# Experts' biases and layer 2's gamma and beta folded into the first product of a two-layer mixture-of-experts kernel, GELUs of 512 columns

## The chip, the cores and the metric

One core of a Trainium2 chip. The metric is device time in microseconds (us) of one execution; smaller is better. The kernel before takes 3586.99 us, the median of 14 runs (3571.68 to 3599.5).

## The reference

Sixteen batches of 512 tokens of width 128 go through six stages. Two kinds of feed-forward layer with 8 experts (each token goes to 2) come twice each, with attention between the first two and a state-space mixer ("mamba") between the last two. All is float32.

```python
x = x + 0.5 * _L0_ffn_ref(_layernorm(x), ...)      # call n = 0
x = x + _L0_attn_ref(_layernorm(x), ...)
x = x + 0.5 * _L0_ffn_ref(_layernorm(x), ...)      # call n = 1
x = x + 0.5 * _L1_ffn_ref(_layernorm(x), ...)      # call n = 2
x = x + _L1_attn_ref(_layernorm(x), ...)           # mamba
x = x + 0.5 * _L1_ffn_ref(_layernorm(x), ...)      # call n = 3

# _L0_ffn_ref, per expert (buf: the rows sent to it, at most a capacity)
h = gelu(einsum('ecd,edf->ecf', buf, W1) + b1, approximate=True)
ye = einsum('ecf,efd->ecd', h, W2) + b2
# _L1_ffn_ref: x is normalized once more inside, then
xn = (x - mu) * rsqrt(var + LN_EPS) * gamma + beta
h = gelu(einsum('bld,edh->eblh', xn, w1) + b1, approximate=False)
out_e = einsum('eblh,ehd->ebld', h, w2) + b2       # combined with the two gates; + x
```

D = 128 is the token width, F = 512 an expert's hidden width (NF = 4 pieces of 128), E = 8 experts. A row that comes out of a layer norm has a sum of zero, so its last number is minus the sum of the other 127.

## The kernel before

Each of the four expert calls n = 0 to 3 is cut into four groups of batches (`GROUPS`: 2, 5, 5, 4 batches, then 2, 4, 5, 5 twice, then 5, 5, 4, 2). A group is one `moe(...)` with these parts:

- `front(b)` (L551 and on) computes the norm's moments of a batch, the normalized and transposed rows, and the router's logits. `routes()` computes, for a whole group, to which slot of a DRAM buffer every row goes. `scatter(b)` (L657, L662) makes the normalized rows on POOL and sends them to `slots` by indirect DMAs, 8 for a batch.
- `blocks()` (L687 and on) runs over the slots in blocks of 256 rows (`BS`); a block belongs to one expert. A group of 2 batches has 15 blocks, of 4 batches 23, of 5 batches 27; 368 in all, 184 for each of the two layers. `fetch(i)` reads the block's expert number into a register and loads that expert's packed row `wb` (first weights, second weights, b1, b2; 1,156 numbers for each partition, L693) and the 256 rows `xs` (L697). `turned(xs)` transposes them on TensorE into `ps_b` (L709) and copies them out as `bl_xT`: on VectorE for layer 1 (L712), on ScalarE with gamma and beta as scale and bias for layer 2 (L714). The first product writes four pieces of 256 columns into two PSUM tiles `ps_h0` and `ps_h1` (L727). Four GELUs of 256 columns, each with its column of b1 as bias, make `hT` (L736). One block later, `second_product` multiplies `hT` with the second weights into `ps_b` (L676), VectorE adds b2 (`yo`, L681), and ScalarE's queue stores the result (L685).
- `back(b)` gathers the results by indirect DMAs on POOL (L775) and adds them to x on VectorE (L767).

`ps_b` is a single PSUM buffer: transposes of a block and second products of the block before alternate in it. `ps_h0` and `ps_h1` are single too. `wb` has three buffers, `xs` three, `hT` two.

At the start, SyncE's queue loads x, then packs both layers' weights in DRAM (`packed`, L419, from four inputs each), with the clearing of the four `slots` buffers (L407) between.

The mamba's `states(b)` (L960 and on) is 16 steps of two scans on VectorE (L978, L987), with exponentials on ScalarE (L984), a product on POOL (L990) and a sum on TensorE (L997).

Two planners set the order. The first, at the end of `macaron_kernel`, keeps a table of tasks with hand-written costs per engine, ranks and dependencies, and writes the instructions in the order that it finds. The lock "blocks" lets only one group's blocks run at a time. The second, `arrange`, is a list scheduler with a cost for every instruction: it sets each engine's whole order anew, the queues of DMAs included, and the order it finds is fixed on every engine.

Of the kernel before, what the change touches and what calls it, by code (L numbers as in the profile page):

```python
# [18 lines left out]
P = 128  # L19
# [18 lines left out]
BS = 256  # L38
LBS = 8
NJ = BS // P  # L40
WIDE = F + NF * D + NF + D


def n_blocks(nb):
# [272 lines left out]
def macaron_kernel(ctx: ExitStack, tc: tile.TileContext, a: dict, out: bass.AP):  # L317
# [95 lines left out]
    for pre, names in (("L0_ffn_", ("W1", "W2", "b1", "b2")), ("L1_ffn_", ("w1", "w2", "b1", "b2"))):  # L413
        t = dram.tile([P, E, WIDE], F32, name=f"packed_{pre}", bufs=1)
        w1d, w2d, b1d, b2d = (a[pre + n] for n in names)
        at = 0
        for src in (w1d, w2d.rearrange("p e f d -> p e (f d)"), b1d, b2d.unsqueeze(0).to_broadcast([P, E, D])):
            n = src.shape[2]
            nc.sync.dma_start(out=t[:, :, at : at + n], in_=src)  # L419
            at += n  # L420
        packed.append(t)
        for s in slots[len(packed) * 2 - 2 : len(packed) * 2]:
            clear(s)

    def mamba_constants():
        nc.scalar.activation(am, am, AF.Exp)
# [114 lines left out]
    def moe(layer, members, n_call):  # L541
# [145 lines left out]
        def blocks():  # L687
            act = AF.Gelu_apprx_tanh if layer == 0 else AF.Gelu
            st["results"] = dram.tile([NBLK * BS, D], F32, name="results", bufs=8)
            def fetch(i):  # L690
                e = nc.sync.value_load(st["expert_of"][0:1, i : i + 1], min_val=0, max_val=E - 1)
                wb = we_p.tile([P, WIDE], F32, name="wb")
                nc.sync.dma_start(  # L693
                    out=wb, in_=packed[layer][:, bass.ds(e, 1), :].rearrange("p o f -> p (o f)")
                )
# [7 lines left out]
                b1b, b2b = wb[:, NF * D : NF * D + NF], wb[:, NF * D + NF :]  # L703
                return w1b, w2b, b1b, b2b, xs

            def turned(xs):
                pt = ps_b.tile([P, BS], F32, name="ps_b")
                for j in range(NJ):
                    nc.tensor.transpose(pt[:, j * P : (j + 1) * P], xs[:, j, :], ident)  # L709
                xT = bl_p.tile([D, BS], F32, name="bl_xT")  # L710
                if layer == 0:
                    nc.vector.tensor_copy(xT, pt)  # L712
                else:
                    nc.scalar.activation(xT, pt, AF.Identity, bias=beta, scale=gamma)  # L714
                return xT

            held, ahead = None, fetch(0)
            unstored = None
            xT = turned(ahead[-1])
            for i in range(nblk):  # L720
                w1b, w2b, b1b, b2b, _ = ahead
                hT = bl_p.tile([P, NF, BS], F32, name="hT")
                ph = [ps_h.tile([P, NF // 2, BS], F32, name=f"ps_h{f}") for f in range(2)]

                nxt = None
                for f in range(NF):
                    nc.tensor.matmul(  # L727
                        ph[f // 2][:, f % 2, :], w1b[:, f * P : (f + 1) * P], xT, start=True, stop=True
                    )
                    if f == NF // 2 - 1 and i + 1 < nblk:  # L730
                        ahead = fetch(i + 1)
                        nxt = turned(ahead[-1])
                xT = nxt

                def gelu(f):
                    return nc.scalar.activation(hT[:, f, :], ph[f // 2][:, f % 2, :], act, bias=b1b[:, f : f + 1])  # L736

                for f in range(NF):
                    gelu(f)

                if unstored is not None:
                    store(*unstored)
                    unstored = None
                if held is not None:
                    unstored = second_product(*held)
                held = hT, w2b, b2b, slice(i * BS, (i + 1) * BS)
                if i == nblk - 1:
                    store(*unstored)
                    store(*second_product(*held))
                yield  # L750
# [291 lines left out]
    n_call = itertools.count()  # L1042
    moes = [
        [moe(n // 2, members, next(n_call)) for members in split(GROUPS[n])] for n in range(4)
    ]
# [66 lines left out]
    for n in range(4):  # L1112
        for g, m in enumerate(moes[n]):
            first, last = m["members"][0], m["members"][-1]
            due = (EARLY, first * PACE - 550, first * PACE - 300, (last + 1) * PACE - 60)[n]
            fronts = [("front", n, b) for b in m["members"]]
            routes = [("routes", n, g)]
            task(
                ("routes", n, g), call(m["routes"], 4, 14, 1, 0, 22), DVE,
                (EARLY - 100 + last + 0.5, EARLY, due - 20, due - 20)[n], fronts, "routes",  # L1120
            )
            task(("scatter", n, g), scatters(m), POOL, due, routes, "scatter")
            task(
                ("blocks", n, g), steps(m["blocks"](), (4.3, 0.5, 2.6, 0, 0)), PE, due + 50,
                [("scatter", n, g)], "blocks",
            )
# [107 lines left out]
```

## Time and profile before

The profiled execution took 3576.5 us by the clock of the runs, of which 3574.8 us are its span from the first instruction to the last. The mean granted TensorE clock is 0.906.

| what | value |
|---|---|
| median of 14 runs | 3586.99 us |
| the profiled execution, and its span | 3576.5 us, 3574.8 us |
| first product, L727, TensorE | 2944 records (two for a matmul), 792.2 us |
| second product, L676, TensorE | 5888 records, 794.7 us |
| activation table loads, ScalarE, all lines | 430 of 1.283 us |
| expert weights `wb` | 368 loads of 578 KB |
| first block's first product starts | 116.87 us |
| first scan of the mamba's batch 0, of batch 2, last scan | 1345 us, 1717 us, 3321 us |

A row of the groups reads: line, engine, operation, tile written and tiles read, shapes, count, then busy time and mean duration of one, and then how long the engine had sat idle just before such instructions and which engine and line ended most of that. Where an engine's instructions overlap, the busy time is less than count times mean. The chain of waits goes back from the last instruction to what released it, step by step; a line's share in it is time that the end waited for.

Until about 1345 us the kernel runs the blocks of n = 0 and n = 1 with the attention, TensorE busy 75 to 80%. From 1717 us, about every 110 us a batch of the mamba is scanned, VectorE busy near 90%, with the blocks of the other calls beside it. After the last scan only the last blocks are left.

### The profile page before, as it was taken

How to read it: one execution, taken by the hardware profiler on the slowest of the kernel's cores; microseconds unless marked ns; L12 is line 12 of the kernel's file. 1: busy time of each engine (PE TensorE's matmuls, PEld its weight loads, DVE VectorE, ACT ScalarE, POOL GpSimd, SP SyncE). 2: the span in 40 equal slices, each digit the busy share in tenths (PEclk: the TensorE clock that was granted, in tenths of full speed). 3: DMA queues.
4: the chain of work that ended last, by engine and by line, in shares of the span. 5: the costliest groups of instructions: out<-in, count | busy, mean ns of one | idle time of the engine just before them, and what ended most of it. 6: DMA issues, size and time to landing. Idle time of an engine off the chain costs nothing.

```text
span 3574.8 us, 45599 instructions
## 1 busy us (share of the span) xinstructions
PE 2784.8 (78%) x13384; PEld 1986.4 (56%) x13384; DVE 2407.9 (67%) x5487; ACT 2151.0 (60%) x3752; POOL 1851.4 (52%) x1557
## 2 busy tenths in 40 slices
PE   3789687775877779897897976899898789764775
PEld 2677566664766655675555642555565256422564
DVE  6715572562753428962897898899879897899412
ACT  2435462552733458874887864789888579742432
POOL 2771504315255434546437378863644984577413
PEclk9999898978989989998999997999999899986898
DMA  9675324424345545654555552555555366433354
GB/s 291 191 226 154 116 68 147 128 63 139 106 144 174 159 143 170 204 169 136 188 174 177 160 167 84 160 172 165 188 184 167 107 189 193 143 121 104 111 167 136
DMA packets 379575, 552.52 MB, mean 155 GB/s; under 512 B 43136, under 2 KB 278336, under 8 KB 379328
## 3 DMA queue, kind: packets, MB, share of 16 engines
q1 hardware_dynamic: 243648, 433.39, 39.3%
q0 software_dynamic: 32768, 67.17, 6.1%
q10 hardware_dynamic: 102912, 49.06, 4.8%
q8 instruction: 107, 1.75, 0.2%
q14 instruction: 140, 1.15, 0.1%
HBM read 448.28 MB, written 110.66 MB: 156 GB/s over the span
## 4 chain that ended last, share of the span: by engine, by line
PE 36%; DVE 28%; issue 10%; POOL 8%; ACT 6%; DMA 5%; another core or an unknown queue 5%; SPq 0%; ACTq 0%; POOLq 0%; DVEq 0%
PE ps_b L676 11%; PE ps_h L727 10%; DVE u L987 6%; DVE u L978 5%; PE ps_s L997 4%; POOL u L990 4%; PE ps_t L907 3%; POOL slots L662 2%; DVE x L767 2%; DVE yo L681 2%; PE ps_b L709 2%; DMA gt<-results,whole 2%; DMA wb<-packed_L_ffn__215 1%; POOL row L657 1%
## 5 line engine op out<-in xcount | busy, mean ns | idle before, releaser
L990 POOL TENSOR_TENSOR u<-u,C 128x1024 f32<-128x1024 f32 x256 | 640.5, 2505 | 530.7 <-DVE u L987 355.9
L736 ACT ACTIVATE hT<-ps_h,wb 128x256 f32<-128x256 f32 x1472 | 601.6, 473 | 516.3 <-PE ps_h L727 289.7
L676 PEld LDWEIGHTS ps_b<-wb,hT 128*128 128x128 f32 x5888 | 762.5, 202 | 193.0 <-issue 80.8
L676 PE MATMUL ps_b<-wb,hT 128*128 128x128 f32 x5888 | 794.7, 288 | 95.0 <-DVE bl_xT L712 39.0
L727 PE MATMUL ps_h<-bl_xT,wb 128*128 128x256 f32 x2944 | 792.2, 400 | 25.4 <-ACT hT L736 13.4
L775 POOL DMA_INDIRECT gt<-results,whole x512 | 520.9, 1017 | 550.4 <-DMA xs<-slots 168.0
L662 POOL DMA_INDIRECT slots<-row,whole x512 | 531.1, 1037 | 510.7 <-issue 251.8
L997 PE MATMUL ps_s<-u,ident 128*128 128x512 f32 x1024 | 552.5, 659 | 153.8 <-POOL u L990 153.3
L727 PEld LDWEIGHTS ps_h<-bl_xT,wb 128*128 128x128 f32 x2944 | 550.8, 202 | 161.7 <-issue 72.1
L987 DVE TENSOR_TENSOR_SCAN u<-ps_a,u 128x512 f32<-128x512 f32 x512 | 602.3, 1208 | 47.5 <-ACT ps_a L984 41.2
L681 DVE TENSOR_TENSOR yo<-ps_b,wb 128x256 f32<-128x256 f32 x368 | 153.9, 418 | 662.9 <-PE ps_b L676 402.8
L978 DVE TENSOR_TENSOR u<-B,dx 128x1024 f32<-128x1024 f32 x256 | 449.1, 1762 | 32.7 <-PE ps_s L997 20.8
L984 ACT ACTIVATE ps_a<-dl,am 128x512 f32<-128x512 f32 x512 | 345.2, 686 | 198.3 <-DVE u L987 175.7
L997 PEld LDWEIGHTS ps_s<-u,ident 128*128 128x128 f32 x1024 | 192.8, 206 | 359.9 <-POOL u L990 215.2
L709 PE MATMUL ps_b<-ident,xs 128*128 128x128 f32 x736 | 164.8, 299 | 230.8 <-DVE yo L681 173.8
L767 DVE SCALAR_TENSOR_TENSOR x<-gt,m,x 128x128 f32<-128x128 f32 x512 | 230.9, 460 | 83.1 <-DMA gt<-results,whole 62.1
L709 PEld LDWEIGHTS ps_b<-ident,xs 128*128 128x128 f32 x736 | 94.9, 148 | 327.7 <-DVE yo L681 220.7
L907 PE MATMUL ps_t<-xT,wc 128*128 128x512 f32 x512 | 243.5, 614 | 21.9 <-ACT cv L910 10.1
L736 ACT ACT_TABLE_LOAD x176 | 225.8, 1283 | 56.4 <-PE ps_h L727 19.9
L657 POOL TENSOR_SCALAR row<-x,q,off 128x128 f32<-128x128 f32 x256 | 157.4, 617 | 124.1 <-DVE off L564 111.5
L984 ACT ACT_TABLE_LOAD x146 | 187.3, 1283 | 13.5 <-DVE yo L681 7.2
L714 ACT ACTIVATE bl_xT<-ps_b,beta,gamma 128x256 f32<-128x256 f32 x184 | 103.2, 561 | 141.7 <-PE ps_b L709 113.2
(170 smaller groups left out, 2891.9 us busy)
## 6 DMA issues: line engine op xcount, KB each, us to landing
wb<-packed_L_ffn__215 SPq DMA_DIRECT2D x184, 578.0 KB
wb<-packed_L_ffn__222 SPq DMA_DIRECT2D x184, 578.0 KB
B<-rows SPq DMA_DIRECT2D x128, 512.0 KB
C<-rows SPq DMA_DIRECT2D x128, 512.0 KB
xs<-slots SPq DMA_DIRECT2D x368, 128.0 KB
results<-yo ACTq DMA_DIRECT2D x368, 128.0 KB
slots<-empty SPq DMA_DIRECT2D x4, 3456.0 KB
slots<-row,whole POOLq DMA_INDIRECT x512
```

The costliest lines, as they stand in the source:

```text
L662: ins = nc.gpsimd.indirect_dma_start(out=dst, out_offset=bass.IndirectOffsetOnAxis(ap=st["whole"][:, k, i : i + 1], axis=0), in_=row, in_o ...
L676: nc.tensor.matmul(py[:, j, :], hT[:, f, j * P : (j + 1) * P], w2b[:, f, :], start=f == 0, stop=f == NF - 1,)
L709: nc.tensor.transpose(pt[:, j * P : (j + 1) * P], xs[:, j, :], ident)
L727: nc.tensor.matmul(ph[f // 2][:, f % 2, :], w1b[:, f * P : (f + 1) * P], xT, start=True, stop=True)
L736: return nc.scalar.activation(hT[:, f, :], ph[f // 2][:, f % 2, :], act, bias=b1b[:, f : f + 1])
L775: nc.gpsimd.indirect_dma_start(out=gt, out_offset=None, in_=st["results"][: nblk * BS, :], in_offset=bass.IndirectOffsetOnAxis(ap=st["whol ...
L907: nc.tensor.matmul(ph, wc[i][:, h, k, :], xT[:, at : at + SEQ], start=k == 0, stop=k == 3)
L978: nc.vector.tensor_tensor(u, bc[0], dx[:, h, :].unsqueeze(1).to_broadcast([P, NCH, SEQ]), ALU.mult)
L984: nc.scalar.activation(da, dl[:, h, :], AF.Exp, scale=am[:, h, n : n + 1])
L987: nc.vector.tensor_tensor_scan(u[:, i, :], da, u[:, i, :], 0.0, ALU.mult, ALU.add)
L990: nc.gpsimd.tensor_tensor(u, u, bc[1], ALU.mult)
L997: nc.tensor.matmul(py[h], ident, u[:, i, :], start=g == 0 and i == 0, stop=g == NS // NCH - 1 and i == NCH - 1,)
```

## The change

It makes the first product carry the biases. The 127 first numbers of a normalized row are copied to one of two fixed tiles `turn` (by turns), in which the row of the last number stays 1. The first weights are made anew on the chip: their last row becomes the bias (and for layer 2 also beta times the weights), the other rows become gamma times the weights, with the last row's weights taken off, since the last number is minus the sum of the others.

- `packed` no longer holds b1, and `WIDE` goes from 1156 to 1152. The host's inputs stay the same. W1 is no longer copied from DRAM to DRAM.
- `first_weights(layer)` makes the new first weights: POOL makes two 128x128 matrices `fold` and, for two experts at a time, a product of b1 with the identity (`diag`); TensorE does two products of 512 columns for each expert; ScalarE copies them out of PSUM and its queue stores two experts at a time to `packed`. For layer 1 this is written at the start, for layer 2 it is a task of the planner, after routes of the last group of n = 0.
- The four GELUs of 256 columns become two of 512 columns, without bias. Layer 2's copy of the transposed rows becomes a plain copy. The planner's cost of a block on ScalarE goes from 2.6 to 2.0, and the blocks of n = 2 and 3 wait for layer 2's weights.

```diff
-WIDE = F + NF * D + NF + D
+WIDE = F + NF * D + D
...
+    turn = []
+    for i in range(2):
+        t = const.tile([P, BS], F32, name=f"turn{i}")
+        nc.gpsimd.memset(t, 1.0)
+        turn.append(t)
+
+    def first_weights(layer):
...
+        fold = s_p.tile([P, 2, P], F32, name="fold", tag="u")
+        nc.gpsimd.affine_select(
+            out=fold[:, 0, :], in_=ident, compare_op=ALU.is_ge, fill=-1.0, base=D - 2, pattern=[[0, P]],
+            channel_multiplier=-1,
+        )
+        if layer == 1:
+            nc.gpsimd.tensor_scalar(fold[:, 0, :], fold[:, 0, :], gamma, None, ALU.mult)
+            nc.gpsimd.tensor_copy(fold[:, 0, D - 1 : D], beta)
...
+        bias = small.tile([P, E, NF], F32, name="bias", bufs=1)
+        nc.sync.dma_start(out=bias, in_=b1)
+        for e in range(0, E, 2):
+            raw = s_p.tile([P, 2, F], F32, name="u")
+            nc.sync.dma_start(out=raw, in_=w1[:, e : e + 2, :])
+            diag = s_p.tile([P, 2, F], F32, name="u")
+            made = s_p.tile([P, 2, F], F32, name="u")
+            nc.gpsimd.tensor_tensor(
+                diag.rearrange("p e (f d) -> p (e f) d", f=NF),
+                bias[:, e : e + 2, :].rearrange("p e f -> p (e f)").unsqueeze(2).to_broadcast([P, 2 * NF, P]),
+                ident.unsqueeze(1).to_broadcast([P, 2 * NF, P]), ALU.mult,
+            )
+            for k in range(2):
+                pt = ps_a.tile([P, F], F32, name="ps_a")
+                nc.tensor.matmul(pt, fold[:, 0, :], raw[:, k, :], start=True, stop=False)
+                nc.tensor.matmul(pt, fold[:, 1, :], diag[:, k, :], start=False, stop=True)
+                nc.scalar.copy(made[:, k, :], pt)
+            nc.scalar.dma_start(out=packed[layer][:, e : e + 2, :F], in_=made)
+
+    first_weights(0)
...
-                xT = bl_p.tile([D, BS], F32, name="bl_xT")
+                xT = turn[next(n_turn) % 2]
                 if layer == 0:
-                    nc.vector.tensor_copy(xT, pt)
+                    nc.vector.tensor_copy(xT[: D - 1], pt[: D - 1])
                 else:
-                    nc.scalar.activation(xT, pt, AF.Identity, bias=beta, scale=gamma)
+                    nc.scalar.copy(xT[: D - 1], pt[: D - 1])
...
-                def gelu(f):
-                    return nc.scalar.activation(hT[:, f, :], ph[f // 2][:, f % 2, :], act, bias=b1b[:, f : f + 1])
-
-                for f in range(NF):
-                    gelu(f)
+                for f in range(2):
+                    nc.scalar.activation(hT[:, f * NF // 2 : (f + 1) * NF // 2, :], ph[f], act)
...
-                ("blocks", n, g), steps(m["blocks"](), (4.3, 0.5, 2.6, 0, 0)), PE, due + 50,
-                [("scatter", n, g)], "blocks",
+                ("blocks", n, g), steps(m["blocks"](), (4.3, 0.5, 2.0, 0, 0)), PE, due + 50,
+                [("scatter", n, g)] + [("weights",)] * (n > 1), "blocks",
...
+    task(("weights",), call(lambda: first_weights(1), 20, 0, 6, 12, 20), PE, EARLY + 500, [("routes", 0, 3)])
```

More of the change, by code (lines that the diff above doesn't have):

```diff
@@ L412, in macaron_kernel @@
     packed = []
-    for pre, names in (("L0_ffn_", ("W1", "W2", "b1", "b2")), ("L1_ffn_", ("w1", "w2", "b1", "b2"))):
+    for i, (pre, w2, b2) in enumerate((("L0_ffn_", "W2", "b2"), ("L1_ffn_", "w2", "b2"))):
         t = dram.tile([P, E, WIDE], F32, name=f"packed_{pre}", bufs=1)
-        w1d, w2d, b1d, b2d = (a[pre + n] for n in names)
-        at = 0
-        for src in (w1d, w2d.rearrange("p e f d -> p e (f d)"), b1d, b2d.unsqueeze(0).to_broadcast([P, E, D])):
+        at = F
+        for src in (a[pre + w2].rearrange("p e f d -> p e (f d)"), a[pre + b2].unsqueeze(0).to_broadcast([P, E, D])):
             n = src.shape[2]
@@ L423, in macaron_kernel @@
             clear(s)
+    turn = []
[4 more added lines that the diff above has]
+    def first_weights(layer):
+        pre = ("L0_ffn_", "L1_ffn_")[layer]
+        w1, b1 = (a[pre + n] for n in (("W1", "b1"), ("w1", "b1"))[layer])
+        fold = s_p.tile([P, 2, P], F32, name="fold", tag="u")
[6 more added lines that the diff above has]
+            nc.gpsimd.tensor_copy(fold[:, 0, D - 1 : D], beta)
+        else:
+            nc.gpsimd.memset(fold[:, 0, D - 1 : D], 0.0)
+        nc.gpsimd.memset(fold[:, 1, :], 0.0)
+        nc.gpsimd.memset(fold[:, 1, D - 1 : D], 1.0)
+        bias = small.tile([P, E, NF], F32, name="bias", bufs=1)
[17 more added lines that the diff above has]
+    first_weights(0)
     def mamba_constants():
@@ L702, in fetch @@
                 w2b = wb[:, : NF * D].rearrange("p (f d) -> p f d", f=NF)
-                b1b, b2b = wb[:, NF * D : NF * D + NF], wb[:, NF * D + NF :]
-                return w1b, w2b, b1b, b2b, xs
+                return w1b, w2b, wb[:, NF * D :], xs
             def turned(xs):
@@ L720, in blocks @@
             for i in range(nblk):
-                w1b, w2b, b1b, b2b, _ = ahead
+                w1b, w2b, b2b, _ = ahead
                 hT = bl_p.tile([P, NF, BS], F32, name="hT")
@@ L1042, in macaron_kernel @@
     n_call = itertools.count()
+    n_turn = itertools.count()
     moes = [
```

## The prediction

> **What bounds the kernel now.** I read the page first: the engines' shares, the chain's shares, the costliest groups.
>
> ```profile
> PE 2784.8 (78%) x13384; PEld 1986.4 (56%) x13384; DVE 2407.9 (67%) x5487; ACT 2151.0 (60%) x3752; POOL 1851.4 (52%) x1557
> PE 36%; DVE 28%; issue 10%; POOL 8%; ACT 6%; DMA 5%; another core or an unknown queue 5%; SPq 0%; ACTq 0%; POOLq 0%; DVEq 0%
> L736 ACT ACTIVATE hT<-ps_h,wb 128x256 f32<-128x256 f32 x1472 | 601.6, 473 | 516.3 <-PE ps_h L727 289.7
> L714 ACT ACTIVATE bl_xT<-ps_b,beta,gamma 128x256 f32<-128x256 f32 x184 | 103.2, 561 | 141.7 <-PE ps_b L709 113.2
> ```
>
> No engine is full and ScalarE (ACT), which the change relieves, holds only 6% of the chain. The GELUs (L736) are ScalarE's largest group, but before them ScalarE sat idle for 516 us, most of it until the first product came: they wait for TensorE (PE), not TensorE for them. So next the windows by stage, which give busy time of PE, weight loads, VectorE (DVE), ACT and POOL, then the granted clock.
>
> ```profile
> 560.00:1250.00 690.00, 520.63 (x3024) 433.59 (x3024) 337.16 (x1342) 319.21 (x692) 271.76 (x314) 0.89 0.45 134
> 1250.00:1717.00 467.00, 390.97 (x1944) 285.65 (x1945) 273.28 (x568) 315.89 (x530) 228.44 (x197) 0.93 0.55 171
> 1717.00:3240.00 1523.00, 1247.65 (x5082) 765.54 (x5080) 1349.93 (x1977) 1158.42 (x1757) 957.68 (x606) 0.92 0.50 158
> 3380.00:3575.00 195.00, 124.10 (x753) 106.79 (x751) 28.17 (x78) 61.54 (x142) 57.11 (x62) 0.86 0.50 148
> ```
>
> Up to 1717 us TensorE leads (84% of 1250 to 1717), then VectorE (89%), at the end TensorE again. Where blocks run alone, the timeline gives their cycle:
>
> ```profile
> 3422.06 0.44 PE L709 MATMUL ps_b<-ident,xs 128*128 128x128 f32 x2 [0.52 <-DVE yo L681]
> 3422.34 1.89 PE L727 MATMUL ps_h<-bl_xT,wb 128*128 128x256 f32 x8
> 3422.60 0.56 ACT L714 ACTIVATE bl_xT<-ps_b,beta,gamma 128x256 f32<-128x256 f32 x1 [1.96 <-PE ps_b L709]
> 3423.45 1.65 ACT L736 ACTIVATE hT<-ps_h,wb 128x256 f32<-128x256 f32 x4 [0.29 <-PE ps_h L727]
> 3424.07 1.95 PE L676 MATMUL ps_b<-wb,hT 128*128 128x128 f32 x16
> 3426.05 0.42 DVE L681 TENSOR_TENSOR yo<-ps_b,wb 128x256 f32<-128x256 f32 x1 [4.04 <-PE ps_b L676]
> 3426.53 0.44 PE L709 MATMUL ps_b<-ident,xs 128*128 128x128 f32 x2 [0.52 <-DVE yo L681]
> ```
>
> The transposes at 3422.06 and 3426.53 are one cycle apart, 4.47 us. It is transposes, first product, second product, then 0.5 us until `yo` frees `ps_b`. GELUs (1.65 us) and the copy (0.56 us) lie under TensorE. There the change gains nothing: shorter GELUs only wait longer.
>
> **The change part by part.** I add it up on the profiled execution's own 3576.5 us, which lies 10.5 us below the median of 3587.0; at the end I put these 10.5 us back. Positions of instructions are from the orders in which the two kernels were built.
>
> *GELUs.* 1472 of 601.6 us busy become 736 of 512 columns. The nearest row is L910, 512 columns from PSUM with a bias, 677 ns: 736 x 0.677 = 498, so 103 us less ScalarE work. *Layer 2's copy*: L869's 256-column copy takes 0.366 against 0.561: 184 x 0.195 = 36 us less. Sixteen new copies of 0.58 cost 9. ScalarE is freed of 130 us, 6%. What of that lies on the path? I summed the chain in order of time by line: `hT` has 31.2 us in 47 pieces, `bl_xT` 10.8 in 22. Scaled by the new durations (498/601.6 and 0.366/0.561) they give 5.4 and 3.8. I take -9. Bounds: 0 (all pieces replaced by another wait) and 6% of ScalarE's whole chain share, 0.06 x 0.06 x 3575 = -13; that the mamba's scans wait less for their exponentials is a rival below. Table loads are 430 in both orders.
>
> The Trainium skill ("Perfetto Trace Analysis", Optimizing Scalar/DVE Operations) says that grouping raises throughput where an engine is saturated, and that breaking instructions up can finish work sooner where it is not. That speaks against this edit, since ScalarE is at 60%. In this trace, however, the first GELU of a pair starts only after both its matmuls, so no early start is lost. Its roughly 51 ns for each ScalarE access to PSUM would make 736 x 0.051 = 38 us of freed ScalarE time, against 103 by the rows, and the term on the path 3 instead of 5.
>
> *wb 2 KB shorter, b1 gone*: `wb` has 92.7 us on the chain (20 pieces), 0.35% of it is 0.3. Nothing. VectorE's copy of 127 rows instead of 128 has the same columns: nothing.
>
> *Layer 1's weights, at the start.* This is the start of before:
>
> ```profile
> 44.57 1.21 POOL L662 DMA_INDIRECT slots<-row,whole  x1 [31.74 <-DVE stat L458]
> 70.13 12.18 SPq L419 DMA_DIRECT2D packed_L_ffn__215<-in_L_ffn_W  x1
> 87.38 1.01 POOL L662 DMA_INDIRECT slots<-row,whole  x1 [21.13 <-issue]
> 107.58 2.67 SPq L693 DMA_DIRECT2D wb<-packed_L_ffn__215  x3
> 116.87 3.62 PE L727 MATMUL ps_h<-bl_xT,wb 128*128 128x256 f32 x8
> ```
>
> The first `wb` waits for all of `packed`, behind the clearing of `slots`, and the first block starts at 116.87. Now four chains of load, POOL product, matmuls, copy and store stand before it. The bias load comes on SyncE's queue after the last clearing, which leaves that queue at 70.13 and, with the queue full, drains by about 86 (estimate from DMA share 1.0 up to 100 us); it lands near 88. POOL's first product waits for it, after 9 of group 0's 16 scatters, which before ran from 44.57 to 66. So 7 scatters, then POOL's second and third product stand behind that wait; POOL's rows give 2.5 us for a product (L990's 128x1024) and 1.3 for a scatter, so group 0's last scatter goes out near 107 instead of 66. On SyncE's queue the fourth raw load stands behind the first `xs`, which waits for that scatter: issued near 110, landed 112.5, four matmuls of 0.86 (two records of 0.43, as L907's 3.44 for eight) to 116, copy and store to 119.5, `wb` landed near 123.5. **+7** (0 if POOL's stop is shorter than that; +20 if the queue drains ten us later). TensorE waits in between too, with fronts of batches 10 to 14 queued behind, but these had until 150. POOL's 20 us delay of group 1's scatters (87.38 to about 148 before) is covered: blocks of group 0 last to about 184.
>
> *Layer 2's weights, amid group 0's blocks.* Sixteen matmuls of 0.86 = 13.8 us on TensorE, which has 0.5 us of idle in each cycle: 12. They come after block 9's first product, at 169.2 before, now 176. POOL has first to send the rest of group 1, 19 rows with two scatters each (one such set every 3.05 us in its timeline), two sets of group 2, then to make `fold` (1.5, from its rows of 0.2 to 0.45) and the product: 112 + 58 + 6 + 1.5 + 2.5 = 180, about 181 with its signal. TensorE waits 5 us with block 8's second product behind it. **+17** (8 with half of it in idle time; 26 if POOL lies another 9 behind). POOL's own 8 products, 20 us, otherwise fall in its idle half.
>
> *The new order.* Before the first scan stand 187 blocks instead of 159: group 2 of n = 1 now runs ahead of n = 2's first group. At batch 2's first scan it is 212 instead of 209, so from there the two run level. Before, batch 0 starts at 1345 and batch 2 at 1717, with 50 blocks between and VectorE at 59%. Now: 28 more blocks first, then two batches at VectorE's pace, (3262 - 1717)/14 = 110 us each (batch 15's first scan is at 3262). At 5.0 us a block (4.47, plus what lies between) that is 1345 + 140 + 220 = 1705: **-12** (-27 at 4.47; +30 at 6.5). After the last scan stand 34 blocks instead of 37, where TensorE is alone: 3 x 4.47 = **-13** (0 if the scatter of that group comes later).
>
> Sum: -9 + 7 + 17 - 12 - 13 = -10. 3576.5 - 10 + 10.5 = 3577.
>
> **The rivals.**
>
> *The mamba starts late and isn't caught up* (slower). The 28 blocks of group 2 of n = 1 now stand before batch 0. For it: 560 to 1250 us holds some 66 blocks in 537 us, 8.1 us each, with attention between, and the clock falls to half in places. Against it: attention is done before these blocks in both orders. At 6.5 us a block batch 2 starts at 1747, +30 instead of -12: 3619. It decides from 5.4 us a block: with the other terms, -9 + 7 + 17 - 13 = +2, so 28 x r + 1565 - 1717 + 2 = 0.
>
> *All of it hidden* (no change). ScalarE's pieces are taken over by another wait, and the terms of the start fall into the waits for group 1 (TensorE idle 5.8 us at 169): -13 from the tail and +13 from what is left of the weights: 3587. For it: ScalarE's small chain share. Against it: TensorE's 84% where the weights are put.
>
> *The scans gain too* (faster by more). In the mamba's stage VectorE waits for exponentials (L984) and other ScalarE lines:
>
> ```profile
> DVE u L987 <- ACT ps_a L984: 33.5, 32, 3.3
> DVE tmp L949 <- ACT tmp L948: 13.3, 2, 11.0
> ```
>
> If the waits between 1717 and 3240 (33.5 + 13.3, and L953's 4.6) go by two thirds, that is 34 more: 3543. Against: only 6% of ScalarE's work goes.
>
> **How the numbers follow.** Forecast 0.36, scans gain too 0.11, hidden 0.12, mamba late 0.41. Predicted 3577. The bounds of the likeliest case alone run from 3555 to 3598; the range reaches to the rivals' times, 3540 to 3625. Less than 0.2% (7 us) can't be told from no change with this kernel. Faster takes the forecast and the gain, less a little that ends within 7 us: 0.45; within 0.13; slower 0.42.
>
> **What would show it.** GELUs of 512 columns at about 0.68 us, ScalarE near 2020 us busy; the cycle at the end still 4.47 us. First block near 123. A wait of TensorE for POOL amid group 0's blocks. The first scan of batch 0 near 1509 and of batch 2 near 1729 (both with the start's +24), and 13 us less than before from the last scan to the end, which was 3575 - 3321 = 254. I am wrong if batch 2 starts after 1745, if a first scan of later batches drifts from 110 us apart, or if the start lies over 20 us late.

## The result, and the profile after

The changed kernel takes 3647.5 us (median of 10 runs, 3634 to 3664) beside 3589.8 us of the kernel before (47 runs): 1.0163 times as long, 95% interval 1.0146 to 1.0180. Two of the 47 runs took over 4200 us and are left out of that ratio. The forecast was 3577 us with a range of 3540 to 3625. The profiled execution took 3652.8 us, with a span (first to last instruction) of 3649.7 us against 3574.8 before, so 75 us are to be found.

ScalarE did what was asked of it, and more. These are the engines' shares and the GELUs' group in the page of the changed kernel:

```profile
PE 2844.5 (78%) x13448; PEld 2021.0 (55%) x13448; DVE 2407.4 (66%) x5487; ACT 1959.3 (54%) x3032; POOL 1863.6 (51%) x1576
L777 ACT ACTIVATE hT<-ps_h 128x512 f32<-128x512 f32 x736 | 426.8, 597 | 668.8 <-PE ps_h L768 446.6
```

ScalarE is busy 192 us less (2151.0 to 1959.3), but ahead of the GELUs it now stands idle for 669 us instead of 516, mostly until their products come: most of the freed time turned into waiting. At the end of the kernel the cycle of a block is what it was. In the timeline of the changed kernel (start, duration, engine, line) the transposes are 3495.43 - 3490.96 = 4.47 us apart:

```profile
3490.96 0.44 PE L750 MATMUL ps_b<-ident,xs 128*128 128x128 f32 x2 [0.52 <-DVE yo L723]
...
3492.36 0.60 ACT L777 ACTIVATE hT<-ps_h 128x512 f32<-128x512 f32 x1
...
3495.43 0.33 PE L750 MATMUL ps_b<-ident,xs 128*128 128x128 f32 x1 [0.52 <-DVE yo L723]
```

The start of the changed kernel, from the timelines of SyncE's queue, POOL and TensorE:

```profile
69.94 10.98 SPq L447 DMA_DIRECT2D bias<-in_L_ffn_b  x1
...
108.43 0.33 SPq L450 DMA_DIRECT2D u<-in_L_ffn_W  x1
...
122.66 2.63 SPq L735 DMA_DIRECT2D wb<-packed_L_ffn__215  x3
84.19 1.90 POOL L453 TENSOR_TENSOR u<-bias,ident 128x1024 f32<-128x1024 f32 x1 [27.71 <-DMA bias<-in_L_ffn_b]
128.74 3.76 PE L768 MATMUL ps_h<-turn,wb 128*128 128x256 f32 x8
```

POOL stands 27.7 us before the bias, the fourth raw load goes out at 108.4 behind the first `xs`, and the first product comes at 128.7 instead of 116.9.

Where the 75 us arise is best seen by batch. The last step of a batch of the mamba on VectorE is two sums into `xc` (L1010 before, L1048 after); the second of them starts, in us:

| end of batch | 0 | 2 | 5 | 9 | 10 | 11 | 15 | span |
|---|---|---|---|---|---|---|---|---|
| before | 1427 | 1814 | 2204 | 2695 | 2798 | 2904 | 3333 | 3575 |
| after | 1660 | 1886 | 2211 | 2723 | 2851 | 3021 | 3427 | 3650 |
| difference | +233 | +72 | +7 | +28 | +53 | +117 | +94 | +75 |

Batch 0 comes 233 us late, and five batches later that is made good. The loss that stays comes from batch 9 on, most of it at batches 10 and 11. The windows of the changed kernel (busy time and count of PE, weight loads, DVE, ACT and POOL, then granted clock, DMA share and GB/s), cut near its own scans, show the place:

```profile
560.00:1250.00 690.00, 522.07 (x2913) 434.43 (x2912) 341.91 (x1364) 267.89 (x497) 268.46 (x312) 0.87 0.44 127
1250.00:1787.00 537.00, 435.56 (x2192) 322.15 (x2191) 293.21 (x615) 305.60 (x468) 267.36 (x226) 0.92 0.55 166
1787.00:2814.00 1027.00, 859.12 (x3662) 544.39 (x3662) 929.21 (x1389) 757.22 (x1041) 625.03 (x403) 0.93 0.53 165
2814.00:2882.00 68.00, 41.91 (x84) 17.57 (x84) 24.43 (x45) 28.60 (x43) 56.54 (x55) 0.75 0.23 75
2882.00:3414.00 532.00, 396.44 (x1355) 219.12 (x1356) 463.34 (x615) 318.07 (x447) 328.83 (x194) 0.85 0.42 134
3414.00:3650.00 236.00, 167.00 (x1017) 142.66 (x1015) 49.54 (x161) 64.67 (x128) 65.65 (x71) 0.88 0.54 152
```

VectorE is at 90% until 2814, then for 68 us at 36%, then at 87%. This is the hole: batch 10's last scan ends at 2815.5, and the next scan starts at 2882.6. The kernel before has no such hole there; its own window over the same stretch:

```profile
2770.00:2882.00 112.00, 77.55 (x166) 32.52 (x166) 100.45 (x105) 62.11 (x94) 101.74 (x66) 0.77 0.33 112
```

VectorE is at 90% in it. The timeline of the changed kernel across the hole (POOL, DVE, PE and ACT lines):

```profile
2773.47 1.13 POOL L813 DMA_INDIRECT gt<-results,whole  x1 [0.35 <-issue]
...
2813.19 2.34 DVE L1025 TENSOR_TENSOR_SCAN u<-ps_a,u 128x512 f32<-128x512 f32 x2
...
2840.08 3.70 PE L945 MATMUL ps_t<-xT,wc 128*128 128x512 f32 x8 [0.68 <-ACT zs L936]
...
2866.95 0.69 ACT L982 ACTIVATE dl<-ps_t,bdt 128x512 f32<-128x512 f32 x1 [0.82 <-PE ps_t L979]
...
2875.13 1.25 DVE L987 SCALAR_TENSOR_TENSOR tmp<-tmp,ex 128x1024 f32<-128x1024 f32 x1 [13.44 <-ACT tmp L986]
...
2882.62 2.34 DVE L1025 TENSOR_TENSOR_SCAN u<-ps_a,u 128x512 f32<-128x512 f32 x2
```

Blocks' first products stop at 2765 and go on at 2886. From the gathers of `back` at 2773 on, batch 11 goes through norm, convolution (2840), step size (2867) and its factors (2875) to its first scan at 2882.6, and batch 10's scans ended at 2815. So batch 11's preparation lies bare. The busiest engine in the hole is POOL (56.54 of 68 us), 33.7 us of that with scatters of rows (L704); whether these make the hole longer was not tried. Why batch 11 comes so late: batch 11 is the first of the last group of n = 2. The order of the groups' blocks, each named by n and its number from 0 (2.3 is the last group of n = 2), was, without n = 0, which is first in both:

```
before: 1.0 1.1 2.0 1.2 2.1 1.3 2.2 2.3 3.0 3.1 3.2 3.3
after:  1.0 1.1 1.2 2.0 2.1 2.2 1.3 3.0 2.3 3.1 3.2 3.3
```

Group 2.3 ends with block 276 before, at about 2528 us, some 260 us ahead of batch 11's scans. After the change it stands behind 3.0 and ends with block 303, at about 2771, when batch 10 has 45 us of scans left. In both traces 303 blocks' first products start ahead of batch 11's first scan, so the count shows nothing of it.

### The profile page after: what moved, and what is told of

The parts are those of the page before. It is cut to its first block, busy times and chain, and to the rows that moved or that the text cites. A ratio compares the mean times of both kernels' runs of the same rounds, so it can differ in the third digit from the quotient of the medians.

```text
span 3649.7 us, 44966 instructions
## 1 busy us (share of the span) xinstructions
PE 2844.5 (78%) x13448; PEld 2021.0 (55%) x13448; DVE 2407.4 (66%) x5487; ACT 1959.3 (54%) x3032; POOL 1863.6 (51%) x1576
## 4 chain that ended last, share of the span: by engine, by line
DVE 19%; PE 15%; issue 6%; DMA 3%; POOL 3%; ACT 3%; another core or an unknown queue 1%; ACTq 0%; DVEq 0%; POOLq 0%; SPq 0%
DVE u L1025 6%; DVE u L1016 5%; PE ps_b L718 4%; PE ps_h L768 3%; PE ps_s L1035 3%; PE ps_t L945 2%; DVE x L805 1%; POOL u L1028 1%; DMA wb<-packed_L_ffn__220 1%; POOL slots L704 1%; DMA gt<-results,whole 1%; POOL gt L813 1%; DVE yo L723 1%; PE ps_b L750 1%
## 5 line engine op out<-in xcount | busy, mean ns | idle before, releaser
L768 PE MATMUL ps_h<-turn,wb 128*128 128x256 f32 x2944 | 800.9, 404 | 33.1 <-ACT hT L777 10.0
L704 POOL DMA_INDIRECT slots<-row,whole x512 | 533.2, 1041 | 517.2 <-issue 334.5
L777 ACT ACTIVATE hT<-ps_h 128x512 f32<-128x512 f32 x736 | 426.8, 597 | 668.8 <-PE ps_h L768 446.6
L1035 PE MATMUL ps_s<-u,ident 128*128 128x512 f32 x1024 | 561.6, 668 | 174.8 <-POOL u L1028 173.6
L768 PEld LDWEIGHTS ps_h<-turn,wb 128*128 128x128 f32 x2944 | 558.0, 204 | 167.4 <-issue 69.8
L699 POOL TENSOR_SCALAR row<-x,q,off 128x128 f32<-128x128 f32 x256 | 147.6, 579 | 96.1 <-DVE off L606 54.3
L945 PEld LDWEIGHTS ps_t<-xT,wc 128*128 128x128 f32 x512 | 96.1, 194 | 134.1 <-issue 102.4
```

What stands on the lines that cost most here:

```text
L704: ins = nc.gpsimd.indirect_dma_start(out=dst, out_offset=bass.IndirectOffsetOnAxis(ap=st["whole"][:, k, i : i + 1], axis=0), in_=row, in_o ...
L768: nc.tensor.matmul(ph[f // 2][:, f % 2, :], w1b[:, f * P : (f + 1) * P], xT, start=True, stop=True)
L777: nc.scalar.activation(hT[:, f * NF // 2 : (f + 1) * NF // 2, :], ph[f], act)
L945: nc.tensor.matmul(ph, wc[i][:, h, k, :], xT[:, at : at + SEQ], start=k == 0, stop=k == 3)
L1035: nc.tensor.matmul(py[h], ident, u[:, i, :], start=g == 0 and i == 0, stop=g == NS // NCH - 1 and i == NCH - 1,)
```

## The experiments

The runs fell on several chips, on which the kernel before took from 3368 to 3618 us beside them; each ratio is against before on the same chip, in brackets its 95% interval. By the fine order of a kernel the text means where single instructions stand when the groups' order is the same.

**Order or edits.** The new order of groups comes from one number, the planner's cost of a block. The first run puts it into the kernel before, the second takes it back in the changed one.

```diff
-("blocks", n, g), steps(m["blocks"](), (4.3, 0.5, 2.6, 0, 0)), PE, due + 50,
+("blocks", n, g), steps(m["blocks"](), (4.3, 0.5, 2.0, 0, 0)), PE, due + 50,
```

> The kernel before with one number changed: the planner's cost of a block on ScalarE, 2.0 in place of 2.6. No instruction differs, only the order: group 2 of n = 1 runs ahead of n = 2's first group, 187 blocks stand before batch 0's first scan instead of 159, and 34 after the last scan instead of 37. Theory 'order': this order is what the change lost by. After's first scan of batch 2 came at 1799 us against 1725, of which its start had left 24; so 50 us and more remain here: 3630 to 3650, about 1.3% slower than before. Theory 'direct edits' (the weights made on the chip and what they displace, +24 measured up to block 40 and +38 more up to block 56): the order alone costs nothing or gains what the prediction said, 3565 to 3590.

Measured: 1.0217 [1.0187, 1.0247]. (In the traces the first scan of batch 2 is at 1784 in the changed kernel and at 1717 before; the expectation's 1799 and 1725 are off.) The order alone, without any edit to an instruction, costs as much as the whole change and more, though on another chip. The hole is there too, from 2625 to 2690 us; the window of this run:

```profile
2625.00:2690.00 65.00, 37.67 (x78) 15.94 (x78) 21.26 (x46) 29.47 (x44) 52.05 (x55) 0.76 0.27 84
```

> The changed kernel with the planner's cost of a block put back to 2.6: all edits of the change, but the groups in the order of before (159 blocks before batch 0's first scan, 209 before batch 2's, 37 after the last). Theory 'order': what is left is the start and the weights, +24 at most, less the GELUs' -9: 3590 to 3605, within 0.5% of before. Theory 'direct edits': as slow as the changed kernel, 3635 to 3660, with batch 2's first scan near 1790.

Measured: 1.0014 [0.9999, 1.0028]. With the old order of groups all edits together can't be told from no change here. Theory "direct edits", by which this run is as slow as the changed kernel, falls; that the edits cost nothing is not shown by it, since the fine order differs too.

The changed kernel itself, on a chip where before took 3584 us:

> The changed kernel itself, beside the others, since these runs are on another chip than the first comparison (before 3379 there, 3590 here). If the parts add up as measured (order +2.2%, all other edits together +0.1%), it is 2.1 to 2.4% slower than before; if other edits gain more in the new order than in the old one, it is nearer the +1.6% of the first comparison.

Measured: 1.0155 [1.0129, 1.0180]. That is nearer the first comparison than the sum of parts, which came from another chip.

**Which half of the order.** The late half alone, in the kernel before, by one more dependency in the planner:

```diff
+    tasks["blocks", 2, 3]["after"].append(("blocks", 3, 0))
```

> The kernel before with one more dependency in the planner: the blocks of n = 2's last group wait until those of n = 3's first group are written. The new order differs from the old in two places: group 2 of n = 1 ahead of n = 2's first group (early: 187 blocks ahead of batch 0's scans, not 159), and n = 2's last group behind n = 3's first (late: batch 11 waits for block 303 instead of 276). This run has only the late one. If the early half costs (the prediction's 28 blocks at more than 5.0 us each, batch 2 at 1799 instead of 1729), it is within 0.4% of before. If the late half costs (a second hole near batches 11 and 12, where the run with the order alone fell from +9 to +79 us behind), it is 1.2 to 2.2% slower.

Measured: 1.0171 [1.0138, 1.0205]. Against the kernel before, whose span was taken on a chip of the same speed, its batches end +9, +8, +4, +11, +105 and +84 us late (batches 0, 2, 9, 10, 11, 15). Nearly the whole loss comes at batch 11. The window there, and VectorE's waits from 2785 to 2885 us (us in total, times, longest):

```profile
2789.00:2880.00 91.00, 57.27 (x155) 28.52 (x153) 36.63 (x85) 46.03 (x76) 70.35 (x74) 0.77 0.35 105
```

```profile
DVE xc L918 <- ACT cv L914: 29.0, 1, 29.0
DVE x L767 <- DMA gt<-results,whole: 18.0, 9, 6.0
```

The window still holds batch 10's last scans, which end at 2795; the next scan starts at 2881. In these 86 us VectorE waits for gathered rows and, 29 us at one stretch, for batch 11's convolution. This is the hole, made by this one dependency.

The early half was tried first in the changed kernel, by the reverse dependency:

```diff
+    tasks["blocks", 3, 0]["after"].append(("blocks", 2, 3))
```

> The changed kernel (cost 2.0, group 2 of n = 1 ahead as in it) with one more dependency in the planner: the blocks of n = 3's first group wait until those of n = 2's last group are written, as they stood before. So the early half of the new order is kept and the late half undone. If the late half is what the change lost by (+1.7% alone), batch 11 doesn't wait, and this is 0.0 to 0.8% slower than before. If the early half costs too, it stays 1.2% and more slower. A mishap can hide the answer: in this order no block stands between the scans of batches 6 to 10, so those 32 blocks go elsewhere, and 37 stay behind the last scan instead of 34 (+13 us).

Measured: 1.0301 [1.0271, 1.0331]. The mishap took place: 1.3 stands behind 2.2, 2.3 needs its results, and no other block may run ahead of 2.3. From 2176 to 2621 us no block's first product starts, and the hole becomes 133 us, in which TensorE runs blocks (107 us busy) and VectorE is at 30%:

```profile
2793.00:2926.00 133.00, 107.13 (x562) 81.52 (x560) 39.94 (x112) 66.02 (x112) 69.19 (x76) 0.92 0.58 176
```

So in this order the late half can't be undone without a greater loss. A clean early half needs 1.3 ahead of 2.2, here in the kernel before with the cost at 2.0:

```diff
+    tasks["blocks", 2, 2]["after"].append(("blocks", 1, 3))
```

> The kernel before with the planner's cost of a block at 2.0 and one more dependency: the blocks of n = 2's third group wait until those of n = 1's last group are written. That leaves only the early half of the new order: 187 blocks ahead of batch 0's scans, but n = 1's last group ahead of n = 2's third and n = 2's last ahead of n = 3's first, as before (303 blocks ahead of batch 11, 37 after the last scan). If the late half made the hole before batch 12, there is no hole here, and the time is 0.5% faster to 0.4% slower than before; the prediction's own term for this half was -12 us, -0.3%. If the early half costs too (batch 2 came 50 us late in the changed kernel, beside the start's 24), it is 1.0 to 1.5% slower.

Measured: 1.0114 [1.0097, 1.0131]. Against the unchanged kernel run further down (before took 3368 and 3371 us on the two chips) its batches 0, 2, 9, 10, 11 and 15 end +175, +27, +15, +15, +25 and +36 us late: no hole, batch 2 27 us late, and a drift of 21 us more from batch 10 on, where the groups stand as before. The time lies in the range expected if the early half costs too (1.0 to 1.5%). But the drift is where the order didn't change, so how much of the 38 us is the early half is judged below.

The whole change in this order, and the same with layer 2's weights made amid the attention:

```diff
-    task(("weights",), call(lambda: first_weights(1), 20, 0, 6, 12, 20), PE, EARLY + 500, [("routes", 0, 3)])
+    task(("weights",), call(lambda: first_weights(1), 20, 0, 6, 12, 20), PE, EARLY + 500, [("routes", 1, 0)])
```

> The changed kernel (cost 2.0) with the same dependency: all of the change, the early half of its order, the late half undone. By the sums so far: start and weights +0.8%, GELUs and copy -0.4 to -0.9%, early half 0: 0.995 to 1.004 of before. If the early half costs, 1.01 and more.

Measured: 1.0077 [1.0063, 1.0091], between the two ranges expected.

> As the run before it, and layer 2's weights are made behind the routes of n = 1's first group, amid the attention, not amid n = 0's blocks. The prediction put 17 us on their place; if that is so and TensorE has idle time amid the attention, this is 0.2 to 0.5% faster than the run before it. If the start's delay is taken up by later waits anyway, the two are level within 0.2%.

Measured: 1.0119 [1.0102, 1.0136]. Both are slower than before, and with the weights moved away from n = 0's blocks, which should have gained, it is 0.4% slower still. What follows tells how little such a difference says.

**How much the fine order counts.** Every cost in the planner moves single instructions too.

> The kernel before, unchanged, for its trace and as a measure of the comparison: 0.998 to 1.002.

Measured: 1.0010 [0.9996, 1.0024].

```diff
-("blocks", n, g), steps(m["blocks"](), (4.3, 0.5, 2.6, 0, 0)), PE, due + 50,
+("blocks", n, g), steps(m["blocks"](), (4.3, 0.5, 2.7, 0, 0)), PE, due + 50,
```

> The kernel before with the planner's cost of a block at 2.7 instead of 2.6: no instruction differs, the groups stand in the order of before (159 blocks ahead of batch 0, 303 ahead of batch 11, 37 after the last scan), only single instructions are moved. If differences of the fine order count for little, within 0.2% of before. If they are worth what the runs planned differently differed by, 0.3 to 0.8% off, either way.

Measured: 1.0104 [1.0083, 1.0124]. No instruction differs and the groups stand as before, and yet it is 1.0% slower. Its batches 2, 9, 10, 11 and 15 end +17, +15, +18, +26 and +40 us late, much like those of the early half alone.

> The changed kernel with the planner's cost of a block at 2.8: all edits of the change, groups in the order of before, the fine order another than at 2.6 (which was 0.1 and 0.3% slower than before on two chips). If the fine order counts for little, 1.000 to 1.004; if it counts for 0.3 to 0.8%, somewhere from 0.994 to 1.010, and then none of the differences under 0.5% between these kernels can be put down to an edit.

Measured: 1.0080 [1.0059, 1.0101], against 1.0014 at 2.6. So a difference of up to 1% between kernels that were planned differently can't be put down to an edit; 1.0% is the largest of the few such differences seen, and no bound. The early half's 1.1% isn't told apart from this. The late half's 1.7% is larger, and nearly all of it lies in its hole.

**The GELUs' size**, four of 256 columns without bias, the cost at 2.6:

```diff
-for f in range(2):
-    nc.scalar.activation(hT[:, f * NF // 2 : (f + 1) * NF // 2, :], ph[f], act)
+for f in range(NF):
+    nc.scalar.activation(hT[:, f, :], ph[f // 2][:, f % 2, :], act)
```

> As the run with the cost put back to 2.6, but the GELUs in four of 256 columns without a bias, so only the size of the GELUs is undone. By the prediction's term for the GELUs (5 us of the 9 on the path) it is 5 us slower than that run; by the rival 'all of it hidden' it is the same within 3 us; if ScalarE held up VectorE's scans (rival 'the scans gain too'), 20 to 35 us slower. ScalarE's busy time should be some 170 us higher (601.6 against 426.8 in GELUs, if the bias itself costs nothing).

Measured: 1.0111 [1.0085, 1.0138], 1.0% above the run with two. But ScalarE's busy time rose by 30 us only (1970.6 to 2000.8), since a GELU of 256 columns without bias takes 385 ns and not 473. This is its group in the page:

```profile
L777 ACT ACTIVATE hT<-ps_h 128x256 f32<-128x256 f32 x1472 | 475.7, 385 | 449.1 <-PE ps_h L768 380.6
```

29 us of time for 30 us of an engine that is idle 40% of the time looks like too much. So two GELUs were planned as four: the list scheduler's table gives a GELU of 512 columns twice the fixed part.

```diff
+if n == NF // 2 * BS and SET_OF.get(getattr(i, "func", None), 9) < 2:
+    return 0.46 + n * 0.0008, 0.53 + n * 0.0008
 return 0.23 + n * 0.0008, 0.3 + n * 0.0008
```

> The changed kernel with the cost of a block at 2.6, and in the list scheduler's table a GELU of 512 columns costs what two of 256 do (0.46 + 0.0008 a column, not 0.23 + 0.0008 a column). On the chip there are two GELUs of 512 columns; only the order is that of four. If the 1.0% by which four GELUs were slower than two came from the longer GELUs themselves, this is as fast as the run with two (+0.1% against before, within 0.3%). If it came from the order that their planned length brought, this is 0.8 to 1.1% slower than before.

Measured: 1.0088 [1.0063, 1.0113], on another chip than the run with two. So both were run again on one:

> The changed kernel with the cost of a block at 2.6 once more, as the base of the three others, which are compared with it on one chip. On the chip where before takes 3379 us it was level with before (1.0014). If that holds on every chip, 0.999 to 1.003 here too; if the chip on which before takes 3584 us shows the start's 24 us and none of the GELUs' gain, it is 1.005 to 1.009 there.

Measured: 1.0026 [1.0008, 1.0043].

> Two GELUs of 512 columns, planned as if they were four (the order of four), beside the run planned as two. If what four GELUs lost (1.0%) lay in their own length, this is level with the run planned as two (within 0.3%). If it lay in the order, this is 0.6 to 1.0% slower than that run.

Measured: 1.0070 [1.0045, 1.0096]. Two GELUs in the order of four lose 0.4% with the same instructions. What is left of the 1.0% is below what the fine order can do, so the worth of the size stays open.

**The making of the weights.** Without it, the cost at 2.6:

```diff
-for src in (a[pre + w2].rearrange("p e f d -> p e (f d)"), ...
+for src in (a[pre + w1], a[pre + w2].rearrange("p e f d -> p e (f d)"), ...
...
-    first_weights(0)
...
-    task(("weights",), call(lambda: first_weights(1), 20, 0, 6, 12, 20), PE, EARLY + 500, [("routes", 0, 3)])
```

> As the run with the cost put back to 2.6, but no weights are made on the chip: the first weights are copied from DRAM to DRAM into the packed rows as in the kernel before. It leaves out the experts' first biases, layer 2's gamma and beta and the last number of each row in the first product. It shows what making the weights costs: by the prediction 24 us (7 at the start, 17 amid group 0's blocks), so it should be 24 us faster than that run, 3570 to 3580, and its first block's first product near 117 us. If the delay is caught up in later waits, it is within 5 us of it.

Measured: 0.9930 [0.9911, 0.9951], 28 us (0.8%) below the run that makes them, and its blocks stand 13 us earlier at the first, 22 at block 16, 23 at block 32 (counted from 0), and 34 at the end. The size is near the 24 us forecast; since the orders differ too, it is no exact price.

Could it be had cheaper? With bias and raw weights loaded ahead of the clearing, into the mamba's buffers:

```diff
+    fetched = {0: fetch_first(0)}
     packed = []
...
-            raw = s_p.tile([P, 2, F], F32, name="u")
-            nc.sync.dma_start(out=raw, in_=w1[:, e : e + 2, :])
+            raw = raws[e // 2]
```

> The changed kernel with the cost of a block at 2.6, and with the bias and the four pieces of raw first weights of layer 1 loaded ahead of the clearing of the slots (into buffers that the mamba uses later), so POOL's products don't stand behind the clearing, and group 0's scatters not behind them; layer 2's weights are loaded and made early too. Theory 'the start and the weights cost what making them displaces' (0.8% by the run without them): most of it comes back: first block's product near 117 us, 0.4 to 0.7% faster than before. Rival: the loads now delay the clearing by as much (2 MB at some 180 GB/s are 11 us), so the first product stays near 127 us, and the time is within 0.3% of the run with the cost at 2.6.

Measured: 1.0160 [1.0138, 1.0182], and the first product at 135 us, later still. POOL made all four products by 41 us, but then (timelines of POOL and SyncE's queue):

```profile
59.16 1.22 POOL L715 DMA_INDIRECT slots<-row,whole  x1 [14.14 <-DVE newton L524]
...
95.12 34.51 SPq L750 DMA_DIRECT2D xs<-slots  x6
130.78 2.80 SPq L746 DMA_DIRECT2D wb<-packed_L_ffn__225  x3
```

Group 0's scatters begin at 59 instead of 44.6 (the line names a step of VectorE; the clearing, now behind the loads, is the likelier cause, and wasn't tried alone), and the first `wb` stands behind six `xs` until 130.8. The wait moved one place on in the queue. This explains the start alone: against before, on a chip of the same speed, block 0's first product comes 18 us late, block 16's 32, block 144's 38 and the last one's 56. What the blocks lose later wasn't followed up, and a fine order of its own may be part of it.

One buffer cleared first, then the raw weights, the other clearings behind, layer 2's weights amid the attention:

```diff
+    clear(slots[0])
+    fetched[0] = fetch_first(0)
+    second_weights(0)
...
     first_weights(0)
+    clear(slots[1])
+    clear(slots[2])
+    clear(slots[3])
```

> The cost at 2.6, and another start: one slots buffer is cleared, then layer 1's bias and raw weights are loaded, then its second weights, and the other three slots buffers are cleared behind them; layer 2's weights move behind the routes of n = 1's first group, amid the attention. Theory: the start costs by what stands in the queues ahead of the first block, so that is gone: first product at 110 to 118 us, no delay at block 16, and 0.4 to 0.8% faster than the run with the cost at 2.6 alone (the run without any making of weights was 0.8% faster). Rival: TensorE's products at 30 to 45 us are followed by the low granted clock that the run with early loads showed (0.50 from 50 to 140 us), and group 0's blocks lose what the loads gain: within 0.3% of the run with the cost at 2.6.

Measured: 1.0035 [1.0017, 1.0053], level with its base (1.0026). The first product came at 135 us, block 16 at 223 (base 227), block 144 at 1253 (1247). The start was not improved. The rival in that expectation, a low clock after TensorE's early work, rests on a misreading that the last section tells of.

No version that computes the whole reference was faster than the kernel before.

## Why the prediction was wrong, step by step

**GELUs and copy, -9.** The mechanism held, ScalarE's size was off: 597 ns for a GELU instead of 677, 192 us freed instead of 130. The nearest row, L910, has a bias, and the edit takes the bias away. The four GELUs without bias show what it costs: (601.6 - 475.7) / 1472 = 86 ns each, so 126 us came from the bias and (475.7 - 426.8) = 49 us from the size. Without a bias the runs show 385 and 597 ns for 256 and 512 columns. The Trainium skill ("ScalarE: Activation LUTs", What ACT_TABLE_LOAD costs) gives 93 ns for each pointer operand and 186 ns + 0.833 ns a column without one: 399 and 612 ns for the two, near what the runs show. An estimate by that page's figures would have put the GELUs at 736 x 0.612 = 450 us, against 427 measured. The other page, which the prediction names, advises breaking instructions up where an unsaturated engine causes bubbles on other engines; the prediction left out that last condition, which ScalarE's 6% of the chain hardly met. The prediction's 38 us of freed ScalarE time, scaled like its other terms, make 31.2 x 38 / 601.6 = 2 on the path, not 3. On the path the -9 was neither shown nor excluded: in the order of before all edits together came to +0.1 and +0.3%.

**wb shorter, nothing.** Not tried alone; nothing in the runs speaks against it.

**Start +7, layer 2's weights +17.** The sum was nearly right (24), its parts were not: the first product came 12 us late, block 16 23 us, and block 40 still 23 us. The chain went as forecast up to the fourth store of made weights (119.0 us, forecast 119.5), but the first `wb` was issued only at 122.7 and the first product came at 128.7, not 123.5. Layer 2's weights then cost 11, not 17: TensorE's wait for POOL before them didn't occur, and their matmuls ran from 184 to 212 us in four pieces between blocks.

**The new order, -12: the step that failed.** The prediction put it: "At batch 2's first scan it is 212 instead of 209, so from there the two run level." They don't. It compared how many blocks stand ahead of a scan, and not which. The same list of positions, read by groups, has 2.3 behind 3.0 after the change, and batch 11 can't start without 2.3. The run with this half alone lost 1.7%, nearly all of it at batch 11, and a hole is in all three traces with 2.3 behind 3.0 compared here (the changed kernel 68 us, the order alone 65, the late half alone 86). So where the prediction had -12 us, the order cost a hole of 68.

The first half of the step was off in size as well. Batch 0's first scan came at 1558 instead of 1345: less the start's 23, the 28 blocks took 190 us, 6.8 each, above the 5.4 named as the turning point. Batch 2's first scan came at 1784, not 1729. But this was made good by batch 5 (+7), so the rival "the mamba starts late and isn't caught up" had the sign and about half the price (3619 is 32 us above the median before, 58 were measured), and not the place.

Two readings in that step were off too. Batch 15's first scan is at 3232 us, not 3262, and 13 intervals lie between it and batch 2's, so a batch took (3232 - 1717)/13 = 117 us, not 110; with that the term is 1345 + 140 + 233 - 1717 = +1 instead of -12. And the stretch from 560 to 1250 us holds 88 blocks' first products in its 690 us, 7.8 each, not 66 in 537. Neither hides the hole: a forecast near 3590 would have missed it as well.

**The tail, -13.** From the last scan to the end it was 254.2 us and is 235.5, so -19, mostly for the reason given: the first of the last 38 blocks (two groups) starts its first product 7 us ahead of the last scan, where before it started 8 us behind it.

**The sum.** With the measured 23 of the start, 68 for the hole and -19 for the tail it makes 72 of 75 us. The agreement is partly luck: the start's 23 can't be followed through to the end, since batches 2 to 9 swing between +7 and +72, and batch 11 itself took longer once it ran. What is shown is the hole; how the rest divides among start, early half and fine order stays open. Two of the three signs named for a wrong forecast came: batch 2 after 1745, and a first scan of a later batch off its pace.

## What to carry to other kernels

When an edit makes a planner lay the work out anew, follow each consumer to its own producer in both orders; the number of instructions ahead of it can stay the same while the one that it needs moves by hundreds of microseconds. Keep the planner's constants fixed to measure the edit, and change them in a run of their own. Before a difference is put down to an edit, find out what the order alone is worth by a change that touches no instruction: here a cost of 2.7 instead of 2.6 was worth 1.0%, more than all the edits together in the order of before (0.1 and 0.3%).

## What the hardware showed unexpectedly

The bias of a GELU costs time: 473 ns with it and 385 without, for the same 256 columns.

The granted clock, the third figure from the end in a window's line, can mislead at the start of a trace. In the windows from 50 to 60 us, the kernel before shows a granted clock of 1.00:

```profile
50.00:60.00 10.00, 5.32 (x20) 3.53 (x18) 4.62 (x30) 3.30 (x7) 7.82 (x9) 1.00 1.02 323
```

and the run with the early loads 0.50:

```profile
50.00:60.00 10.00, 3.87 (x14) 3.29 (x14) 8.64 (x43) 0.00 (x0) 0.84 (x1) 0.50 1.03 302
```

Yet the same eight router matmuls take as long in both, in the timeline of before

```profile
55.86 1.88 PE L579 MATMUL ps_t<-wg,xT 128*128 128x8 f32 x8 [0.68 <-issue]
```

and in that of the run with early loads:

```profile
58.20 1.88 PE L632 MATMUL ps_t<-wg,xT 128*128 128x8 f32 x8 [0.36 <-DVE pos L693]
```

In that run they took 1.06 us at 45 us, after TensorE had been busy from 30 to 40, with 0.92 shown from 40 to 50. In the kernel before they still take 1.88 us at 102.6 us, with 1.00 shown in every window up to there, and the first change of clock that its trace records lies at 122 us. So both ran slowly between 55 and 60 us, the early loads didn't cost the clock there, and ahead of the first recorded change a duration is to be trusted more than the column.
